# A feed-forward's bias product in four row groups, gelus in pairs, and a new order of its pipelined step

## The chip, the core and the metric

The kernel runs on one NeuronCore of a Trainium2 chip. The metric is the device time of one execution in microseconds (us), the median of several runs. The core has five engines that matter here, each with its own instruction stream: TensorE (PE in the profile; its weight loads are PEld), VectorE (DVE), ScalarE (ACT), GpSimd (POOL) and SyncE (SP, which issues DMAs). [...]

## The reference

Two blocks are applied to x of 8 x 256 x 512. The first adds a convolution-like mixing and then a quantised feed-forward; the second adds a cross attention and a mixture of experts. The change is in the feed-forward of the first block:

```python
def _activation_quant(x):
    scale = 127.0 / jnp.clip(jnp.max(jnp.abs(x), axis=-1, keepdims=True), EPS_ACT)
    return jnp.clip(jnp.round(x * scale), -128, 127) / scale
def _bitlinear(x, w, b):
    xn = _layer_norm(x)
    xq = _activation_quant(xn)
    wq = _weight_quant(w)          # round(w / scale) in {-1, 0, 1}, times scale
    return jnp.einsum('bsd,fd->bsf', xq, wq) + b
h = _bitlinear(x, w1, b1)          # 512 -> 2048
h = jax.nn.gelu(h, approximate=False)
return _bitlinear(h, w2, b2)       # 2048 -> 512
```

So each row is normalised, rounded to integers with a scale of its own, multiplied by a ternary matrix, given a bias, put through a gelu, and then the same again with the second matrix.

## The kernel before

The 2048 rows stay in SBUF as 16 tiles of 128 rows (xs). The kernel has stages: the mixing (to about 193 us of the profiled span), the feed-forward (to about 337 us), the attention, and the experts.

**The feed-forward** works on pairs of tiles, `Pair` (L286), pairs 0 to 7. A pair goes through these methods, each of which issues instructions on one or two engines:

- `moments` (L296, VectorE; the root on GpSimd, `root` L274), `rounded` (L305, VectorE): centres the rows, finds the largest, scales and rounds into xc. L315 is its last instruction.
- `split` (L360, GpSimd): the bias has to be added ahead of a multiplication by the row's scale s1, so it is divided by it: u = 1/s1 is split into three bf16 parts, the bias b1 also (`bias_parts` L240), and the nine products of parts are a matmul of nine rows. The parts of u go to u9 (L366), those of b1 to b1k.
- `turn_x` (L373): eight transposes on TensorE (L171, written as f_xT), moved to xq by ScalarE (L376). `turn_u` (L378): u9 transposed (L382), moved to ub by ScalarE (L384).
- `product(i, half)` (L397): for tile i of the pair and one half (1024 columns) of the hidden layer, eight matmuls (L404) and then two of the bias (L411), into hp, a PSUM tile of two banks. Its tag "conv" has two buffers.
- `gelu(i, half)` (L416, ScalarE): hp to hs in SBUF, with the row sums as a by-product in hsum (L417; it shows as two rows, the second an ACTIVATION_READ_ACCUMULATOR). `hidden` is product and gelu.
- `mean` (L422): from the sums the mean of the gelu's rows, two small VectorE instructions (hm, L425 and L115); then ScalarE centres hs[1] (L427). `centre` (L429): VectorE centres hs[0] (L431).
- `squares` (L435, ScalarE, L439) and `largest` (L443, VectorE, L444) for each tile; `scales` (L448; VectorE, root on GpSimd); `scales_back` (L454, VectorE); `rounded_back` (L460, VectorE, two instructions L462).
- `turn_back(i, half)` (L467): eight transposes (L171, f_hT) and their eviction by ScalarE (L479).
- `back(i)` (L484): sixteen matmuls of the second product (L488). `update(i)` (L493, VectorE, L496) adds it to xs; `add_bias` (L498, two GpSimd adds of the second bias, L500).

**What sets the order.** Everything from L752 to L1211 lies in `in_order(tc)` (L58): on TensorE, VectorE, ScalarE and GpSimd each, instructions run in the order in which the program issues them. So the order is written by hand. Pairs are pipelined: in step g of the loop at L1079 the pair `p` = g has its hidden layer computed, `mid` = g - 1 has its hidden layer's scale computed, `last` = g - 2 goes through the second product, `left` = g - 3 has its last tile finished, and `coming` = g + 1 is normalised and rounded. Pairs 0 and 1 have a run-in ahead of the loop (L1014 to L1078). Step 8 has an order of its own (L1111 to L1146), in which the attention begins; step 9 is the last.

In step g (2 < g < 8) the order ends with these calls, and then comes `left.back(1)` of the next step:

```python
        if p:
            p.hidden(1, 1)
        if mid:
            mid.scales_back()
        prepare(3)
        if coming:
            coming.turn_x()
        if p:
            p.mean()
        if mid:
            mid.rounded_back()
```

PSUM holds, beside "conv", two buffers of "tr" (all transposes) and two of "mm" (second product).

The parts of b1 are brought to b1k by DMAs that ScalarE's queue issues (L248, L251), in the mixing stage: its loop over 16 groups of heads (L779) calls `next(bias_rows)` in groups 9, 10 and 12 (L813).

## Time and profile before

| | |
|---|---|
| runs (3) | median 1145.42 us, 1143.35 to 1147.33 |
| the profiled execution's own time | 1143.72 us |
| its span, first to last instruction | 1141.9 us |
| mean granted clock of TensorE | 0.995 |
| busy, share of the span: PE, PEld, DVE, ACT, POOL | 96%, 58%, 60%, 46%, 39% |
| 0 to 190 us: PE, DVE, ACT, POOL busy | 170.63, 168.71, 100.00, 144.96 |
| 190 to 345 us: PE, DVE, ACT, POOL busy | 147.21, 130.07, 127.39, 62.13 |
| L404: matmuls, busy, mean | 256, 61.8 us, 386 ns |
| L411: matmuls, busy, mean | 64, 19.5 us, 387 ns |
| L417: gelus, busy, mean | 32, 38.5 us, 1204 ns |
| L251: DMAs issued, median time to issue | 3, 282 ns |

The span is counted from the first to the last instruction; times inside it are from its start. Matmuls are pipelined, so one that lasts 386 ns starts 216 ns after the one before it; a sum is made from start to start. "Idle before" is what an engine waited ahead of an instruction, with the instruction that ended the wait.

### The profile page before, as it was taken

To read this page: it belongs to the slowest core of one execution; us is meant where nothing else is said; L and a number is where in the kernel's file an instruction comes from. 1 tells how busy PE (TensorE), PEld (TensorE's weight loads), DVE (VectorE), ACT (ScalarE), POOL (GpSimd) and SP (SyncE) were. 2 spreads that over 40 slices of the span, in tenths; PEclk is the share of its full clock that TensorE was granted. 3 is DMA by queue.
4 is the path that set the end of the run, shared out by engine and by line. 5 is a ranking of instruction groups with operands and counts; after the bars stand their busy time and mean duration, and the time that the engine had idled before them with its cause. 6 is when DMAs were issued, how large, how long until landed. Compare 5 with 4: busy or idle time off the path is not lost.

```text
span 1141.9 us, 16502 instructions
## 1 busy us (share of the span) xinstructions
PE 1099.7 (96%) x5885; PEld 662.1 (58%) x5885; DVE 686.2 (60%) x1507; ACT 519.6 (46%) x1173; POOL 443.0 (39%) x501
## 2 busy tenths in 40 slices
PE   4999998899999999999999998999999999999997
PEld 3777776445545555555555555654466676675443
DVE  5998999898866565765757657637612222212452
ACT  4437645788984555656556566621011121111000
POOL 5787887225531243433434334412770000000650
PEclk9999999999999999999999999999999999999999
DMA  8424520799500100000000010052669999997571
GB/s 272 156 75 143 162 75 20 239 307 290 145 1 19 38 1 1 20 20 1 20 7 13 2 37 1 1 195 93 239 217 297 303 329 338 299 315 231 157 248 40
DMA packets 122780, 153.26 MB, mean 134 GB/s; under 512 B 7481, under 2 KB 81273, under 8 KB 122178
## 3 DMA queue, kind: packets, MB, share of 16 engines
q1 hardware_dynamic: 108608, 116.49, 32.2%
q10 hardware_dynamic: 8962, 18.85, 4.6%
q0 software_dynamic: 5120, 16.78, 4.4%
q8 instruction: 49, 0.80, 0.3%
q14 instruction: 41, 0.34, 0.1%
HBM read 107.66 MB, written 44.43 MB: 133 GB/s over the span
## 4 chain that ended last, share of the span: by engine, by line
PE 75%; DVE 18%; ACT 2%; POOL 2%; issue 2%; DMA 0%; ACTq 0%; POOLq 0%; DVEq 0%
PE r_h L1726 10%; PE gu L1541 10%; PE y L708 5%; PE v_mm L880 5%; PE r_po L1742 5%; PE q_mm L880 5%; PE po L1563 5%; PE f_op L488 4%; PE pt L1281 4%; PE k_mm L880 3%; PE f_hp L404 3%; PE fo L1312 3%; DVE mx L1253 2%; PE sc L1245 2%; PE o L1300 2%
## 5 line engine op out<-in xcount | busy, mean ns | idle before, releaser
L1270 POOL TENSOR_TENSOR pr<-pr,rden 128x1024 f32<-128x1024 f32 x64 | 121.1, 1893 | 218.9 <-DVE rden L1268 212.4
L708 PE MATMUL y<-kv,tp 128*128 128x288 f32 x640 | 161.7, 409 | 5.2 <-DVE wl L731 5.1
L708 PEld LDWEIGHTS y<-kv,tp 128*128 128x128 f32 x640 | 119.3, 190 | 42.3 <-PE y L708 10.1
L1261 ACT ACTIVATE pr<-sc,mx 128x256 f32<-128x256 f32 x256 | 118.3, 483 | 8.2 <-DVE mx L1253 7.2
L1884 POOL DMA_INDIRECT yg<-yd,slot x32 | 33.4, 1043 | 222.2 <-PE gu L1541 204.4
L1726 PE MATMUL r_h<-r_xT,r_gu 128*128 128x256 f32 x512 | 113.5, 380 | 0.0
L1726 PEld LDWEIGHTS r_h<-r_xT,r_gu 128*128 128x128 f32 x512 | 97.1, 190 | 20.4 <-issue 8.0
L1253 DVE TENSOR_REDUCE mx<-sc 128x4 f32<-128x1024 f32 x64 | 77.5, 1213 | 4.8 <-PE sc L1245 4.8
L1733 DVE SCALAR_TENSOR_TENSOR r_y<-r_h,eb,r_ge 128x256 f32<-128x256 f32 x32 | 15.5, 484 | 95.5 <-PE r_h L1726 95.5
L1281 PE MATMUL pt<-ident,pr 128*128 128x128 f32 x512 | 70.5, 281 | 2.3 <-POOL pr L1270 1.4
L1286 ACT COPY pts<-pt 128x512 f32<-128x512 f32 x64 | 37.8, 590 | 68.2 <-PE pt L1281 68.1
L1281 PEld LDWEIGHTS pt<-ident,pr 128*128 128x128 f32 x512 | 55.8, 142 | 20.1 <-issue 15.1
L404 PE MATMUL f_hp<-w1q,f_xq 128*128 128x512 bf16 x256 | 61.8, 386 | 5.5 <-ACT f_h L417 2.9
L1732 ACT ACTIVATE r_ge<-r_h,gb 128x256 f32<-128x256 f32 x32 | 15.1, 473 | 108.9 <-PE r_h L1726 108.9
L646 POOL TENSOR_TENSOR kv<-kx 128x2048 f32<-128x2048 f32 x16 | 57.6, 3600 | 12.8 <-ACT kx L632 12.8
L1312 PE MATMUL fo<-Wo_sb,oT 128*128 128x512 f32 x128 | 58.0, 596 | 1.2 <-ACT oT L1304 1.1
L880 PE MATMUL k_mm<-Wk_sb,cx 128*128 128x512 f32 x128 | 58.1, 598 | 0.6
L488 PE MATMUL f_op<-w2q,f_hq 128*128 128x512 bf16 x256 | 57.9, 379 | 0.0
L880 PE MATMUL v_mm<-Wv_sb,cx 128*128 128x512 f32 x128 | 57.7, 594 | 0.0
L1742 PE MATMUL r_po<-r_w,r_y 128*128 128x512 f32 x128 | 57.7, 594 | 0.0
L880 PE MATMUL q_mm<-Wq_sb,xT 128*128 128x512 f32 x128 | 57.6, 593 | 0.0
L1553 ACT ACTIVATE ge<-gu,gb 128x512 f32<-128x512 f32 x16 | 11.0, 687 | 100.6 <-PE gu L1541 98.0
(486 smaller groups left out, 2114.4 us busy)
## 6 DMA issues: line engine op xcount, KB each, us to landing
xd<-blank SPq DMA_DIRECT2D x1, 15360.0 KB, 59.5
tp<-kpd SPq DMA_DIRECT2D x32, 256.0 KB, 3.3
r_gu<-in_rg SPq DMA_DIRECT2D x16, 512.0 KB, 6.4
r_gu<-in_rw SPq DMA_DIRECT2D x16, 512.0 KB, 6.6
r_w<-in_rw SPq DMA_DIRECT2D x16, 512.0 KB, 6.7
r_xr<-xd SPq DMA_DIRECT2D x16, 512.0 KB, 6.7
yd<-r_yo ACTq DMA_DIRECT2D x32, 256.0 KB, 5.7
yd<-blank SPq DMA_DIRECT2D x1, 6144.0 KB, 78.3
```

The costliest lines, as they stand in the source:

```text
L404: nc.tensor.matmul(dst, lhsT=self.xq[:, i, c, :], rhs=w1q[:, c, cols], start=(c == 0), stop=False)
L488: nc.tensor.matmul(op, lhsT=self.hq[i][:, c, :], rhs=w2q[:, c, :], start=(c == 0), stop=(c == FC - 1))
L708: nc.tensor.matmul(y[:, ll, :, 0:PAIRS], lhsT=tp[:, dl : dl + P], rhs=view(kv, (m0 * G + hh) * PAIRS, [[G * PAIRS, B], [1, PAIRS]]), start ...
L880: nc.tensor.matmul(t, lhsT=lT[:, c, i * P : (i + 1) * P], rhs=w[:, c, :], start=(c == 0), stop=(c == DC - 1),)
L1253: nc.vector.tensor_reduce(self.mx, self.sc.rearrange("p r c k -> p (r c) k"), AX.X, ALU.max, negate=True)
L1261: nc.scalar.activation(self.pr[:, h // 2, h % 2, :], self.sc[:, h // 2, h % 2, :], AF.Exp, bias=self.mx[:, h : h + 1], accum_out=self.den[ ...
L1270: nc.gpsimd.tensor_tensor(flat, flat, rden.unsqueeze(2).to_broadcast([P, 4, S]), ALU.mult)
L1281: nc.tensor.transpose(pt[:, cc, k, :], self.pr[:, rr, cc, k * P : (k + 1) * P], ident)
L1312: nc.tensor.matmul(fo, lhsT=oT[:, c, :], rhs=wsb["Wo"][:, c, :], start=(c == 0), stop=(c == DC - 1))
L1541: nc.tensor.matmul(ps, lhsT=w[0][:, c, k, f * P : (f + 1) * P], rhs=xTs[tb][:, c, :], start=(c == 0), stop=(c == DC - 1),)
L1726: nc.tensor.matmul(ps, lhsT=self.w[0][:, c, k, f * P : (f + 1) * P], rhs=self.xT[:, c, 0:n], start=(c == 0), stop=(c == DC - 1),)
L1742: nc.tensor.matmul(po, lhsT=self.y[:, f, i * P : (i + 1) * P], rhs=self.w[1][:, f, :], start=(f == 0), stop=(f == EC - 1),)
```

## The change

- **Bias parts.** Before, the nine rows of parts lie in partitions 0 to 8 and the bias product of each 512 columns is a matmul over all 128 partitions. After, the nine rows of b1k for columns 512 r to 512 r + 511 lie in partitions 32 r to 32 r + 8 (r = 0 to 3), u9 holds its nine rows four times, 32 apart, and `parts(i)` issues four matmuls of 32 rows each, one per group of 32 rows of the array, each into a PSUM bank of its own. All four of a tile come together, after both halves of the tile. GpSimd writes u9 with two small copies per part, where it was one; the DMAs to b1k are twelve smaller ones where there were three, in groups 11, 12 and 13 of the mixing.
- **A tile's halves.** `product(i, 0)` and `product(i, 1)` both precede `parts(i)`, so both buffers of "conv" belong to one tile. `gelu(i)` issues the tile's two gelus one after the other.
- **The step.** `turns` and the interleaving inside a product are gone. `parts(0)` and `gelu(0)` follow `last.turn_back(0, 1)`; `mid.squares(1)` follows them; `product(1, 0)` follows `last.back(0)`, then `last.turn_back(1, 1)`; `product(1, 1)` and `parts(1)` come where `hidden(1, 1)` was; `gelu(1)` comes after `coming.turn_x()`. Pairs 0 and 1 are rewritten in the same way.

```diff
         for i in range(3):
-            nc.scalar.dma_start(b1k[3 * i : 3 * i + 3, :], b1d)
+            for r in range(4):
+                row = 32 * r + 3 * i
+                nc.scalar.dma_start(b1k[row : row + 3, bass.ts(r, D)], b1d[:, bass.ts(r, D)])
+            yield
...
-                nc.gpsimd.tensor_copy(
-                    u9[:, :, 3 * j : 3 * j + 3],
-                    up[:, j, :].unsqueeze(2).to_broadcast([P, 2, 3]),
-                )
+                for i in range(2):
+                    nc.gpsimd.tensor_copy(
+                        u9[:, i, :].rearrange("p (r k) -> p r k", r=4)[:, :, 3 * j : 3 * j + 3],
+                        up[:, j, i : i + 1].unsqueeze(2).to_broadcast([P, 4, 3]),
+                    )
...
+        def product(self, i, half):
+
+            if half == 0:
+                self.hp = []
             hp = pp.tile([P, FF // 2], F32, tag="conv", name=f"{self.nm}_hp{i}{half}")
-            self.hp = hp
+            self.hp.append(hp)
...
+        def parts(self, i):
+
+            for r in range(4):
+                rows = slice(32 * r, 32 * r + 32)
                 nc.tensor.matmul(
-                    hp[:, q * D : (q + 1) * D], lhsT=self.ub[:, i, :], rhs=b1k[:, cols],
-                    start=False, stop=True,
+                    self.hp[r // 2][:, bass.ts(r % 2, D)], lhsT=self.ub[rows, i, :],
+                    rhs=b1k[rows, bass.ts(r, D)], start=False, stop=True,
                 )
...
+        def gelu(self, i):
+            for half in range(2):
+                nc.scalar.activation(
+                    self.hs[i][:, bass.ts(half, FF // 2)], self.hp[half], AF.Gelu, bias=zero,
+                    scale=self.s1[:, i : i + 1], accum_out=self.hsum[:, i, half : half + 1],
+                )
+
+        def hidden(self, i):
+
+            for half in range(2):
+                self.product(i, half)
+            self.parts(i)
+            self.gelu(i)
...
-        if g in (9, 10, 12):
+        if g in (9, 10, 11, 12, 13):
             next(bias_rows, None)
...
-    one.hidden(0, 0)
-    one.hidden(0, 1)
+    one.hidden(0)
...
-    one.hidden(1, 0)
+    one.product(1, 0)
     more_mixed()
-    one.hidden(1, 1)
+    one.product(1, 1)
+    one.parts(1)
+    one.gelu(1)
...
-    two.hidden(0, 0)
+    two.hidden(0)
     three.moments()
     one.largest(0)
     one.squares(0)
-    two.hidden(0, 1)
     three.rounded()
     three.split()
-    two.hidden(1, 0)
+    two.product(1, 0)
...
     two.product(1, 1)
+    two.parts(1)
     one.scales_back()
     three.turn_x()
     three.turn_u()
-    two.gelu(1, 1)
+    two.gelu(1)
...
-        def turns():
-
+        if p:
+            p.product(0, 0)
             if g > 2:
                 p.turn_u()
-            mid.squares(1)
-            if g > 2:
-                last.turn(0, 0)
-
-        if p:
-            p.hidden(0, 0, turns)
-        if g == 2:
-            p.hidden(0, 1)
-        if g == 2 or not p:
-            last.turn(0, 0)
-        last.turned(0, 0)
+            else:
+                p.product(0, 1)
+                p.parts(0)
+                p.gelu(0)
+        last.turn_back(0, 0)
...
         if p and g > 2:
-            p.hidden(0, 1)
+            p.product(0, 1)
         last.turn_back(0, 1)
...
-        if p:
-            p.hidden(1, 0)
+        if p and g > 2:
+            p.parts(0)
+            p.gelu(0)
+        if mid:
+            mid.squares(1)
         last.turn_back(1, 0)
         last.back(0)
+        if p:
+            p.product(1, 0)
+        last.turn_back(1, 1)
...
-        last.turn_back(1, 1)
         if p:
-            p.hidden(1, 1)
+            p.product(1, 1)
+            p.parts(1)
         if mid:
             mid.scales_back()
         prepare(3)
         if coming:
             coming.turn_x()
         if p:
+            p.gelu(1)
             p.mean()
```

More of the change, by code (lines that the diff above doesn't have):

```diff
@@ L390, in turn_u @@
             self.hsum = stat.tile([P, 2, 2], F32, tag="hsum", name=nm + "_hsum")
-        def hidden(self, i, half, between=None):
-            self.product(i, half, between)
-            self.gelu(i, half)
-        def product(self, i, half, between=None):
+        def product(self, i, half):
+            if half == 0:
+                self.hp = []
             hp = pp.tile([P, FF // 2], F32, tag="conv", name=f"{self.nm}_hp{i}{half}")
-            self.hp = hp
+            self.hp.append(hp)
             for q in range(2):
                 cols = bass.ts(2 * half + q, D)
-                dst = hp[:, q * D : (q + 1) * D]
                 for c in range(DC):
                     nc.tensor.matmul(
-                        dst, lhsT=self.xq[:, i, c, :], rhs=w1q[:, c, cols], start=(c == 0), stop=False
-                    )
-            if between:
-                between()
-            for q in range(2):
-                cols = bass.ts(2 * half + q, D)
+                        hp[:, bass.ts(q, D)], lhsT=self.xq[:, i, c, :], rhs=w1q[:, c, cols],
+                        start=(c == 0), stop=False,
+                    )
+        def parts(self, i):
+            for r in range(4):
+                rows = slice(32 * r, 32 * r + 32)
                 nc.tensor.matmul(
-                    hp[:, q * D : (q + 1) * D], lhsT=self.ub[:, i, :], rhs=b1k[:, cols],
-                    start=False, stop=True,
-                )
-        def gelu(self, i, half):
-            nc.scalar.activation(
-                self.hs[i][:, bass.ts(half, FF // 2)], self.hp, AF.Gelu, bias=zero,
-                scale=self.s1[:, i : i + 1], accum_out=self.hsum[:, i, half : half + 1],
-            )
+                    self.hp[r // 2][:, bass.ts(r % 2, D)], lhsT=self.ub[rows, i, :],
+                    rhs=b1k[rows, bass.ts(r, D)], start=False, stop=True,
+                )
+        def gelu(self, i):
[9 more added lines that the diff above has]
+            self.gelu(i)
         def mean(self):
```

## The prediction, made before the change was run

> **What bounds the kernel now.** I read the busy shares first (TensorE 96%), then the table of busy times by stretch for the feed-forward steps, and then the timelines of the engines inside one step. The table (us; then busy us and instruction counts of TensorE, its weight loads, VectorE, ScalarE, GpSimd; then granted clock, DMA share, GB/s) has for one step of the loop:

> ```profile
> 263.80:282.10 18.30, 18.28 (x116) 9.54 (x115) 16.54 (x32) 16.22 (x19) 8.23 (x21) 1.00 1.05 289
> ```

> TensorE is full: a step lasts 18.30 us because its matmuls do. But VectorE has 16.5 and ScalarE 16.2 of the same 18.30, so a saving on TensorE is worth little before another engine is late. What that engine is, the timelines of VectorE and ScalarE say (start, us, instruction, idle before it):

> ```profile
> 275.15 0.87 DVE L315 TENSOR_SCALAR f_xc<-f_xc,f5q_qs 128x512 f32<-128x512 f32 x2
> 278.00 0.16 DVE L266 TENSOR_TENSOR f3hq_a<-f_hmax,f3h_r 128x2 f32<-128x2 f32 x1 [1.24 <-POOL f3h_r L283]
> 278.81 0.15 DVE L425 TENSOR_TENSOR f_hm<-f_hsum 128x2 f32<-128x2 f32 x1
> 279.10 2.47 DVE L462 TENSOR_SCALAR f_h<-f_h,f3hq_qs 128x2048 f32<-128x2048 f32 x2
> 292.82 0.88 DVE L315 TENSOR_SCALAR f_xc<-f_xc,f6q_qs 128x512 f32<-128x512 f32 x2
> ```
> ```profile
> 276.48 1.20 ACT L417 ACTIVATE f_h<-f_hp,zero,f_s 128x1024 f32<-128x1024 f32 x1 [0.54 <-PE f_hp L411]
> 277.58 0.19 ACT L417 ACTIVATION_READ_ACCUMULATOR f_h<-f_hp,zero,f_s 128x1 f32 x1
> 277.67 1.10 ACT L376 ACTIVATE f_xq<-f_xT,nhalf 128x1024 bf16<-128x1024 f16 x1
> 279.27 2.00 ACT L427 ACTIVATE f_h<-f_h,f_hm 128x2048 f32<-128x2048 f32 x1 [0.49 <-DVE f_hm L115]
> ```

> VectorE's own round: rounding of the coming pair (L315, ends 276.02), L425 (hm, which needs the gelu's sums) 2.8 later, and 14.9 from hm to the end of the next rounding (278.81 to 293.70). Together 17.7, under 18.3, and hm does not wait: the last gelu's sum is there at 277.77, a microsecond early, because that gelu runs **ahead** of xq (L376).

> **The change, part by part.**

> *Bias parts in row groups.* Before, a tile's four bias matmuls cost 4 x 0.216 = 0.86 (L411: two in 0.43, start to start). The scores of the later attention are four 32-row matmuls side by side:

> ```profile
> 414.25 3.60 PE L1312 MATMUL fo<-Wo_sb,oT 128*128 128x512 f32 x8
> 417.78 1.15 PE L1245 MATMUL sc<-kT_T,qT_T 32*128 32x256 f32 x16
> 418.85 1.09 PE L1281 MATMUL pt<-ident,pr 128*128 128x128 f32 x8
> ```

> The sixteen take 1.07 to the next start; sixteen at full height and this width would take 3.49 (eight of twice the width, L880, take 3.49). So four cost about 1.23 of one, and four bias matmuls about 0.27; the ends are 0.22 and 0.86. TensorE is spared 0.59 a tile, 9.5 us over 16 tiles; a step of two tiles then needs 17.1.

> The scores begin 0.04 after the last full-height matmul should end (414.25 + 3.49). [...] At 0.04 a switch, 32 switches would cost 1.3 of the 9.5; no more than that can be read off this trace.

> *Nine more small DMAs (L251)* on ScalarE's queue, 0.28 each: 1.1 us more in each of two groups of the mixing stage, 0.3 in a third. ScalarE idles there 1.8 to 6.6 us a group before the next kx copy (waiting for its DMA), which hides them; without that cover it is 2.5 at most. Nothing is gained. I take 0. They land long before 196 us, the first use.

> *GpSimd's split:* 11 instructions instead of 8. At its measured starts (L365 to L371, 0.15 to 0.26 apart) it lasts 2.1 instead of 1.7, and starts 1.9 after the rounding's end (295.58 against 293.70), so it ends at 4.1. Behind it stands the bias add L500.

> *The new order of the step: the part that decides.* L417's last two gelus are now issued **after** the coming pair's turn_x. ScalarE runs in program order, so they queue behind xq, xq behind the eight transposes, and these behind the rounding. hm waits for both gelus, and VectorE's 14.9 us of work stand behind hm. So a new ring closes. From the rounding's end R:

> - to the transposes' start 0.1; from there to xq 0.65 (208.42 to 209.07);
> - xq to gelu 0.99 (220.14 to the next start, 221.13);
> - two gelus with the second's sum 2.45 (below: 227.99 to 230.44), to hm 0.03: hm at R + 4.2, where it was R + 2.8;
> - hm to the next rounding's end 14.9.

> ```profile
> 227.99 1.18 ACT L417 ACTIVATE f_h<-f_hp,zero,f_s 128x1024 f32<-128x1024 f32 x1
> 229.17 1.19 ACT L417 ACTIVATE f_h<-f_hp,zero,f_s 128x1024 f32<-128x1024 f32 x1
> 230.25 0.19 ACT L417 ACTIVATION_READ_ACCUMULATOR f_h<-f_hp,zero,f_s 128x1 f32 x1
> ```

> **19.1 us a round.** TensorE, at 17.1, now stands 2 us in each step in front of the transposes L171. ScalarE keeps up: its last square ends 0.1 to 1.5 us before xq can start.

> *A collision.* The add L500 follows the split, at R + 4.1; hm comes at R + 4.2. What the two do to each other is in this pair of rows, GpSimd's and VectorE's:

> ```profile
> 241.37 1.26 POOL L500 TENSOR_TENSOR xs<-xs,b2b 128x512 f32<-128x512 f32 x1
> ```
> ```profile
> 241.39 1.27 DVE L115 SCALAR_TENSOR_TENSOR f_hm<-f_hm,ones 128x2 f32<-128x2 f32 x1
> ```

> A 0.16 us instruction took 1.27, until the add ended. If this happens in each round, it is 20.2 (add's end 5.35, second hm 0.2, then 14.6 from L462 on). If the split ends later than the ring assumes (ScalarE's square late by 0.5), its last small casts are pushed between the two L462 and the add behind the next L431, as at 281.58, at no cost. I take two rounds of each; the ends are four of 19.1 and four of 20.2. [...]

> *Four rounds* (hm of pair 3 to hm of pair 6 count from that of pair 2, g = 3 to 6; after that no pair is coming). Before: L425 at 241.19 and 314.45, 73.3. After: 2 x 19.1 + 2 x 20.2 = 78.6. **+5.3** (+3.1 to +7.5).

> *Run-in.* Pairs 0 and 1 gain about 0.4 at the start, where VectorE's adds L624 set the pace. Then both gelus of a tile run together, so the next tile's first half finds its PSUM buffer taken (TensorE waits 1.4 at 213.8), pair 0's two squares end at 220.3 (were at 220.2), and xq, ub, two gelus follow: hm of pair 1 at 224.0 (was 223.5). In g = 2 the gelus and two evictions (2.36 + 2.0) now stand ahead of the square of hs[1], and the square of hs[0] behind the eviction of the last transposes: it ends 239.4, then xq 1.0 and gelus 2.45, hm at 242.8. This is at full clock. Before, a pause of 2.63 halved the clock for what followed:

> ```profile
> 229.31 3.23 PE L404 MATMUL f_hp<-w1q,f_xq 128*128 128x512 bf16 x8 [2.63 <-ACT f_h L417]
> ```

> and 1.7 us went. After, the pause is 2.2; the price is 0 to 1.7, I take half. hm of pair 2 at 243.6: **+2.4** (+1.6 to +3.3).

> *Run-out.* In g = 7 nothing is coming, the gelus wait for the square alone, and hm of pair 7 comes 17.5 to 18.0 after that of pair 6 (was 333.81 - 314.45 = 19.4): **-1.4** (to -1.9). From there, g = 8 and all later stages are the same code and move as a block.

> **Sum.** 2.4 + 5.3 - 1.4 = +6.3. The profiled execution took 1143.72 (span 1141.9, 1.8 around it), so it would take 1150.0; the median of the runs is 1145.42, 1.7 above it, and with the same shift I forecast **1151.7**. Its ends are +2.8 and +9.7.

> **Rivals.**

> - *Faster.* TensorE's spared time is collected: VectorE runs its own round of 17.7, TensorE needs 17.1, and each of four steps falls from 18.3 to 17.7, with 1.2 more in g = 7: -3.6, 1141.8. For it: no idle of TensorE in five steps, and every step it gives back is on the chain of waits. It decides if hm comes within 3.1 us of the rounding's end; the rows make it 4.2, since xq and the two gelus alone are 3.4. Chance 0.12.
> - *No change (within 0.3%, 3.4 us, about what a measurement of this kernel can tell).* The ring holds at 19.1 with no collision, and the run-in is hidden, for VectorE has waits of 1.9 (L266 at 222.70) to spare: 0 to 0.5 + 3.1 - 1.9, about +1.5, 1146.9. Chance 0.16.
> - *Worse.* The collision in each round, and the clock halved after each pause: transposes 0.45 later in four rounds, 9.7 + 1.8 = +11.5, 1156.9. For it: the pause is 2 to 3 us, at the 2.63 that halved it once. Chance 0.12.
> - *The row groups do not run side by side.* TensorE then needs 18.3 a step, still under 19.1, and the time is the forecast's; it is no separate case.

> The forecast itself has 0.60. Slower by over 0.3%: 0.60 + 0.12 = 0.72; same 0.16; faster 0.12. The range from 1146.0 to 1157.0 leaves out the faster case and little else.

> **What would show it.** Right: L376 ahead of two L417 in ScalarE's row, L425 idle 1.4 us or longer with ACT f_h L417 as its releaser (before: 0.57, once), transposes L171 of f_xT preceded by 2 us of idle TensorE released by DVE f_xc L315, steps of 19 to 20.3, L411 four at a time in about 0.3. Wrong: TensorE without gaps from 245 on, or steps under 18.3; or hm early, which would mean that ScalarE's order is not what I read from the code. The collision shows as an L425 or L115 of 1.2 us beside L500; the clock as a granted clock under 0.9 in the steps.

## The result, and the profile after

After the change the kernel takes **1159.9 us** (median of 4 runs, 1157.89 to 1162.25); the kernel before, beside it, 1144.49. The ratio is 1.0128, with a 95% interval of 1.0110 to 1.0146: slower, as forecast, but by 15.4 us where 6.3 were forecast, and outside the range that was given. The profiled execution took 1162.25, the longest of the four; its span is 1160.5, TensorE's mean granted clock 0.992.

Landmarks of the two profiled executions (start, us from the span's start; hm is L425 before and L437 after) say where the time comes from. A pair's hm marks the middle of its step, so hm to hm is one round of the loop; the run-in is what lies ahead of hm of pair 2, the run-out is from hm of pair 6 to hm of pair 7:

| | before | after | moved by | the prediction |
|---|---|---|---|---|
| hm of pair 2 | 241.19 | 246.78 | +5.6 | +2.4 |
| hm of pair 6 (four rounds) | 314.45 | 325.73 | +11.3 | +7.7 |
| hm of pair 7 | 333.81 | 344.81 | +11.0 | +6.3 |
| first xTp of the attention | 343.3 | 355.8 | +12.5 | +6.3 |
| rank, start of the routing | 781.2 | 792.1 | +10.9 | +6.3 |
| first r_h, end of the routing | 842.3 | 860.9 | +18.6 | +6.3 |

**The rounds.** One round of the loop, hm to hm, in the table of busy times by stretch (columns as before):

```profile
265.69:285.76 20.07, 17.81 (x116) 8.82 (x115) 17.16 (x33) 16.54 (x19) 9.88 (x28) 1.00 1.05 289
```

TensorE is no longer full: 17.81 of 20.07. The timelines of VectorE, ScalarE, GpSimd and TensorE around that hm, in this order (start, us, instruction, idle before it and what ended it):

```profile
280.87 0.88 DVE L319 TENSOR_SCALAR f_xc<-f_xc,f5q_qs 128x512 f32<-128x512 f32 x2
...
285.76 1.25 DVE L437 TENSOR_TENSOR f_hm<-f_hsum 128x2 f32<-128x2 f32 x1 [1.15 <-ACT f_h L422]
```
```profile
282.24 1.11 ACT L381 ACTIVATE f_xq<-f_xT,nhalf 128x1024 bf16<-128x1024 f16 x1 [1.10 <-PE f_xT L171]
283.25 1.20 ACT L422 ACTIVATE f_h<-f_hp,zero,f_s 128x1024 f32<-128x1024 f32 x1
...
284.43 1.20 ACT L422 ACTIVATE f_h<-f_hp,zero,f_s 128x1024 f32<-128x1024 f32 x1
```
```profile
285.72 1.27 POOL L512 TENSOR_TENSOR xs<-xs,b2b 128x512 f32<-128x512 f32 x1
```
```profile
279.67 0.39 PE L415 MATMUL f_hp<-b1k,f_ub 32*128 32x512 bf16 x4
281.41 0.79 PE L171 MATMUL f_xT<-ident,f_xc 128*128 128x128 f16 x8 [1.35 <-DVE f_xc L319]
```

This is the ring as forecast: rounding (ends 281.7), transposes, xq, two gelus, hm, which waits 1.15 for the second gelu. Then the collision: GpSimd's add has started 0.04 before hm, and hm takes 1.25 in place of 0.15. This is not a wait ahead of an instruction, as the 1.15 is, but an instruction that lasts 1.1 longer: GpSimd's add held VectorE up without a wait.

The rounds are 18.9, 20.1, 20.0 and 20.0, 79.0 in all (forecast 78.6; before 73.3). The hm of 1.25 above lengthens the round that starts with it, and so does the next one; these are the third and the fourth. The round shown, the second, is long for another reason, near its start (VectorE, then GpSimd):

```profile
268.43 2.37 DVE L443 TENSOR_SCALAR f_h<-f_h,f_hm 128x2048 f32<-128x2048 f32 x1
```
```profile
268.45 1.27 POOL L512 TENSOR_TENSOR xs<-xs,b2b 128x512 f32<-128x512 f32 x1
```

Here the split was late, and the add came behind it, the outcome that the prediction put at no cost. But the centring L443 took 2.37 in place of 1.28 beside the add. In the first round the split was late too, and there the add took 2.31 and L443 its usual 1.27. The rows of the two rounds differ by one more VectorE instruction ahead of L443 in the second (L1100, 0.15, which only g = 4 has); that it decides who is held up is not shown. The kernel before has the same 2.37 in that step (L431 at 262.72).

**The clock.** TensorE in g = 2, then in g = 8:

```profile
223.12 5.30 PE L406 MATMUL f_hp<-w1q,f_xq 128*128 128x512 bf16 x16 [2.66 <-ACT f_h L422]
...
232.32 0.61 PE L171 MATMUL f_hT<-ident,f_h 128*128 128x128 f16 x8 [2.57 <-ACT f_hq L491]
232.77 5.30 PE L500 MATMUL f_op<-w2q,f_hq 128*128 128x512 bf16 x16
```
```profile
346.42 1.03 PE L171 MATMUL f_hT<-ident,f_h 128*128 128x128 f16 x8 [3.08 <-DVE f_h L474]
347.25 4.77 PE L892 MATMUL k_mm<-Wk_sb,cx 128*128 128x512 f32 x8
```

Sixteen such matmuls take 3.62 at full clock and these eight take 3.65 (both are shown below, in the changed kernel's second execution). The granted clock is 0.50 from 224.5 to 226.5, from 234 to 236 and from 347.3 to 349, and 1.00 in all four rounds. So three pauses, of 2.66, 2.57 and 3.08, are each followed by 1.5 to 1.7 us of lost time on TensorE.

**The run-out.** Nothing is coming in this step, and still two of VectorE's small instructions stand beside an add (GpSimd's adds start at 325.69 and 342.90):

```profile
325.73 1.24 DVE L437 TENSOR_TENSOR f_hm<-f_hsum 128x2 f32<-128x2 f32 x1 [1.15 <-ACT f_h L422]
...
342.98 1.20 DVE L270 TENSOR_TENSOR f6hq_a<-f_hmax,f6h_r 128x2 f32<-128x2 f32 x1 [1.26 <-POOL f6h_r L287]
```

**The end.** In the routing VectorE has two long waits (7.44 ahead of L1581 at 835.81, which the profile puts down to TensorE, and 6.96 at 845.61, put down to something outside the core) that it does not have in the profile before. That code is the same in both kernels; whether the wait belongs to the change was a question for the runs.

### The profile page after: what moved, and what is told of

It reads as the page before. It is cut to its first block, busy times and chain, and to the rows that moved or that the text cites. A ratio compares the mean times of both kernels' runs of the same rounds, so it can differ in the third digit from the quotient of the medians.

```text
span 1160.5 us, 16538 instructions
## 1 busy us (share of the span) xinstructions
PE 1097.9 (95%) x5885; PEld 656.7 (57%) x5885; DVE 688.9 (59%) x1507; ACT 520.7 (45%) x1173; POOL 440.7 (38%) x525
## 4 chain that ended last, share of the span: by engine, by line
PE 69%; DVE 21%; ACT 4%; POOL 2%; issue 2%; another core or an unknown queue 1%; DMA 0%; ACTq 0%; POOLq 0%; DVEq 0%
PE r_h L1740 10%; PE gu L1555 10%; PE y L720 5%; PE v_mm L892 5%; PE r_po L1756 5%; PE q_mm L892 5%; PE po L1577 4%; PE k_mm L892 3%; PE pt L1295 3%; PE fo L1326 3%; PE f_op L500 2%; DVE mx L1267 2%; PE sc L1259 2%; PE f_hp L406 2%; PE o L1314 2%
## 5 line engine op out<-in xcount | busy, mean ns | idle before, releaser
L500 PE MATMUL f_op<-w2q,f_hq 128*128 128x512 bf16 x256 | 59.6, 387 | 0.0
L1555 PE MATMUL gu<-xT,s_gu 128*128 128x512 f32 x128 | 56.2, 594 | 0.0
```

What stands on the lines that cost most here:

```text
L500: nc.tensor.matmul(op, lhsT=self.hq[i][:, c, :], rhs=w2q[:, c, :], start=(c == 0), stop=(c == FC - 1))
L1555: nc.tensor.matmul(ps, lhsT=w[0][:, c, k, f * P : (f + 1) * P], rhs=xTs[tb][:, c, :], start=(c == 0), stop=(c == DC - 1),)
```

## The experiments

In all, 15 kernels ran, in four groups on four chips, each beside the kernel before (1141.88, 1145.22, 1142.07 and 1145.22 us). "Rounds" is hm of pair 2 to hm of pair 6.

**The changed kernel again.** No edit.

> The changed kernel itself once more, beside the other experiments. After the feed-forward its product of rank came 10.9 us later than in the kernel before, but the whole execution took 18.5 us more, because the routing stage waited 7.4 and 7.0 us on VectorE for transfers of rows (dxs), which four other executions with the same stage did not do. If that wait belongs to one run and not to the change: 1152 to 1155, rank to first r_h 61 us, ratio about 1.010. If it belongs to the changed kernel: 1158 to 1162 again, and rank to r_h 68 to 69.

1158.4 (1155.36 to 1158.63), ratio 1.0106 (1.0086 to 1.0127): the loss is there again. From rank to r_h 64.5: neither 61 nor 68. All four kernels of that chip had 64.5 to 66.7, the one with the order of before too (h, below, 65.0); all eight on two other chips had 61.1 or 61.2, whatever their order. And the kernel before without its bias adds (o, below), on a fourth chip, shows the same wait (VectorE):

```profile
814.21 0.75 DVE L1553 SCALAR_TENSOR_TENSOR yT<-gu,eb,ge 128x512 f32<-128x512 f32 x1 [6.23 <-remote]
826.74 0.69 DVE L1566 TENSOR_TENSOR xs<-xs,po 128x512 f32<-128x512 f32 x1 [9.67 <-remote]
```

The medians of the kernel before agree: 1141.88 and 1142.07 on the two chips with 61.1 or 61.2, 1145.22 on both of the others. So these waits vary between chips and executions, and are not the change's. The clock varies too: the same pauses as above, in this execution of the same kernel, cost nothing in two cases of three (the first was followed by 5.30 again):

```profile
232.88 0.61 PE L171 MATMUL f_hT<-ident,f_h 128*128 128x128 f16 x8 [2.58 <-ACT f_hq L491]
233.32 3.62 PE L500 MATMUL f_op<-w2q,f_hq 128*128 128x512 bf16 x16
...
345.37 0.62 PE L171 MATMUL f_hT<-ident,f_h 128*128 128x128 f16 x8 [3.09 <-DVE f_h L474]
345.83 3.65 PE L892 MATMUL k_mm<-Wk_sb,cx 128*128 128x512 f32 x8
```

**c: dummy matmuls in the three pauses.**

```diff
+    def warm(n, name):
+        ps = pp.tile([P, D], F32, tag="mm", bufs=2, name=name)
+        for _ in range(n):
+            nc.tensor.matmul(ps, lhsT=w1q[:, 0, 0:P], rhs=w1q[:, 0, 0:D], start=True, stop=True)
...
+        if g == 2:
+            warm(11, "warm0")
         if p:
             p.product(0, 0)
...
+        if g == 2:
+            warm(10, "warm1")
         last.turn_back(1, 0)
...
             left.back(1)
+            warm(12, "warm2")
             mid.centre()
```

> The changed kernel with matmuls that nobody reads put into three pauses of TensorE: eleven ahead of the first product of g = 2, ten ahead of the third group of transposes of g = 2, twelve ahead of the first transposes of g = 8 (0.22 us each). Theory: these pauses of 2.6, 2.6 and 3.1 us halve TensorE's clock, which costs 1.8, 1.7 and 1.5 us after them; kept busy, the clock stays full and the time falls by 4 to 5 us, to 1155 to 1156; the first product of g = 2 lasts 3.5 for sixteen instead of 5.3, hm of pair 2 comes 3.4 earlier than 246.8. Rival (the run-in is late because of its order alone, the clock is covered by waits): within 1 us of 1159.9.

1149.9, ratio 1.0073 (1.0056 to 1.0091); hm of pair 2 comes 3.5 earlier than in the first profile after, first xTp at 350.8, 5.0 earlier than in the first and 2.5 earlier than in the second. The product behind the dummies is at full speed:

```profile
220.18 2.54 PE L1025 MATMUL warm<-w1q 128*128 128x512 bf16 x11
223.01 3.62 PE L406 MATMUL f_hp<-w1q,f_xq 128*128 128x512 bf16 x16 [0.29 <-ACT f_h L422]
```

So the clock costs the changed kernel up to 5 us in an execution. With it gone hm of pair 2 is at 243.30, 2.1 later than before, where the prediction's terms without the clock make +1.6; 1.4 of the 2.1 lies between hm of pair 1 and that of pair 2 (19.1 against 17.7).

**d: the kernel before, with nothing but both gelus of tile 1 behind turn_x.**

```diff
         if p:
-            p.hidden(1, 0)
+            p.product(1, 0)
+            hp0 = p.hp
...
-            p.hidden(1, 1)
+            p.product(1, 1)
+            hp1 = p.hp
...
             coming.turn_x()
         if p:
+            p.hp = hp0
+            p.gelu(1, 0)
+            p.hp = hp1
+            p.gelu(1, 1)
             p.mean()
```

> The kernel before (bias at full height, old order), with one part of the change alone: the two gelus of a pair's second tile are issued after the coming pair's turn_x. Theory of the ring: hm at 4.2 us after the rounding's end instead of 2.8; the four rounds grow from 73.3 to between 76.4 and 81, and the time from 1144.5 by 2 to 8 us, to 1146.5 to 1152.5, with hm waiting for the gelu in each of steps 3 to 6. Rival (the order of these gelus is harmless, the loss comes from the rest of the new order): within 1.5 us of 1144.5.

1147.01, ratio 1.0039 (1.0025 to 1.0053). Rounds 77.7 in place of 73.3, and hm waits for the gelu and for an add:

```profile
283.42 0.85 DVE L425 TENSOR_TENSOR f_hm<-f_hsum 128x2 f32<-128x2 f32 x1 [1.16 <-ACT f_h L417]
```

The late gelus alone, in the old order and at full-height bias parts, and the collision that they bring (0.7 in three of the rounds), make most of the loss in the rounds (4.4 of 5.7).

**a: the changed kernel with tile 1's gelus ahead of turn_x.**

```diff
             p.parts(1)
+            p.gelu(1)
...
             coming.turn_x()
         if p:
-            p.gelu(1)
             p.mean()
```

> The changed kernel, but in the loop the gelus of a pair's second tile are issued right after their bias parts, ahead of the coming pair's turn_x (the old place); all else as changed. Theory (ring: rounding, transposes, xq, two gelus, hm, VectorE's 14.9 us): the ring opens, VectorE's own round of 17.7 or TensorE's 17.1 bounds, so the four rounds from hm of pair 2 to hm of pair 6 fall from 79.0 to 71 to 73.5, hm no longer waits for a gelu, and the time falls by 6 to 9 us from the changed kernel's 1159.9, to 1151 to 1154. Rival (the halved TensorE clock in g = 2 and g = 8 and the small GpSimd copies made the loss, not the order): rounds stay at 19 to 20 and the time within 2 us of 1159.9.

1154.06, ratio 1.0106 (1.0089 to 1.0123): almost nothing is won. hm no longer waits, but the rounds are 19.7, where the rival had them. TensorE, then VectorE, show a second ring, which my theory lacked:

```profile
288.22 0.46 PE L387 MATMUL f_uT<-ident,u 128*128 128x128 f32 x2 [1.62 <-POOL u L371]
```
```profile
300.98 0.16 DVE L119 SCALAR_TENSOR_TENSOR f4h_ve<-f_hss,ln_eps 128x2 f32<-128x2 f32 x1 [1.93 <-ACT f_junk L451]
```

ScalarE's square of hs[0] now ends last; behind it come GpSimd's root, and behind that the split, whose last small operations each take 1.1 to 1.3 beside VectorE's roundings in place of 0.2 to 0.3. So turn_u is late, and with it ub, both evictions, parts(0), the gelus and again the square.

**b: four bias matmuls at full height, in the changed order.**

```diff
-                    self.hp[r // 2][:, bass.ts(r % 2, D)], lhsT=self.ub[rows, i, :],
-                    rhs=b1k[rows, bass.ts(r, D)], start=False, stop=True,
+                    self.hp[r // 2][:, bass.ts(r % 2, D)], lhsT=self.ub[:, i, :],
+                    rhs=b1k[:, bass.ts(r, D)], start=False, stop=True,
```

> The changed kernel, but the four bias matmuls of a tile run at full height, all 128 rows, one after the other (the other rows of b1k are zero, so the sum is the same). Theory of the ring: TensorE stands 1.3 to 2 us in each late round in front of the transposes, so 0.55 us more per tile is hidden in the loop; rounds of 18.9 to 20.1 as before, time within 3 us of 1159.9 (the run-in and the run-out may pay for some tiles). Rival (the row groups are worth what they spare on TensorE): 16 x 0.55 = 9 us slower, 1169.

1153.73, ratio 1.0100 (1.0080 to 1.0120), rounds 79.4, against 79.0 in both executions of the changed kernel: while the rings set the pace, the row groups are worth 0.1 a round.

**h: the row groups in the order of before,** two at a time.

```diff
-                    hp[:, q * D : (q + 1) * D], lhsT=self.ub[:, i, :], rhs=b1k[:, cols],
+                    hp[:, q * D : (q + 1) * D], lhsT=self.ub[32 * r : 32 * r + 32, i, :],
+                    rhs=b1k[32 * r : 32 * r + 32, bass.ts(r, D)],
```

> The kernel before, its order kept, with nothing of the change but the bias parts in row groups: two at a time, beside each other, behind each half's product. Two side by side take 0.24 to 0.28 where two at full height took 0.43: 0.3 to 0.4 us a step and half of it a tile, so 0.6 to 0.7 a step of TensorE's 18.3. Theory: the steps are bound by TensorE, so that rounds 3 to 6 fall from 18.3 to 17.7 (VectorE's own round of 17.7 is next), and the time falls by 2 to 3.5 us, ratio 0.997 to 0.998. Rival: VectorE or the split (11 casts instead of 8, which push the add) is late instead, and nothing is gained or 1 to 2 us lost.

1146.23, ratio 1.0010 (0.9992 to 1.0028), rounds 73.7 (18.4 each). Nothing is gained, as the rival had it, but not for the rival's reason: TensorE is still full (18.3 of 18.4 us of a round). Its rows show why:

```profile
286.15 1.89 PE L408 MATMUL f_hp<-w1q,f_xq 128*128 128x512 bf16 x8
287.97 0.39 PE L416 MATMUL f_hp<-b1k,f_ub 32*128 32x512 bf16 x2
288.29 0.62 PE L171 MATMUL f_hT<-ident,f_h 128*128 128x128 f16 x8
```

The product takes 1.82 to the start of the parts (1.73 before, when full-height matmuls followed), and two parts 0.32, where the two of before took 0.43: 2.14 against 2.16. Four together, in the changed kernel, take the same 0.32 to 0.33 (291.19 to 291.51). So two at a time save nothing, and four at a time 4.32 less 3.88 (1.73 + 1.82 + 0.33), 0.44 a tile.

**e and l: the adds moved in the changed kernel.** In e `left.add_bias()` comes after `coming.moments()`; l only turns the two adds round:

```diff
-            for T in self.T:
+            for T in self.T[::-1]:
                 nc.gpsimd.tensor_tensor(T, T, b2b, ALU.add)
```

> The changed kernel with GpSimd's two bias adds issued after the coming pair's moments, so that no add stands behind the split when hm comes. Theory of the collision (in three of four rounds an add holds VectorE's 0.16 us instruction for 1.25): these three rounds fall from 20.0 to 18.9, hm of pair 6 and all later landmarks come 3 us earlier, and hm lasts 0.15. Rival, found in the kernel with the gelu first: a second ring through the square of hs[0], its root on GpSimd and the split holds the rounds near 19.7 whatever the add does: then at most 1 us is won.

> The changed kernel with nothing but the order of GpSimd's two adds turned round: tile 1's first. It must wait for the update of tile 1, so both run some 6 us after hm, beside VectorE's statistics, which the trace shows at their usual 0.68 beside such an add, and not beside the 2x tensor_scalars. Theory of the collision: three rounds of 20.0 become 18.9, hm lasts 0.15, hm of pair 6 and rank come 3.3 us earlier than in the same kernel with the old order. Rival: the second ring (square of hs[0], root, split, turn_u) is as long as the first: 1 us or less.

e: 1161.72, ratio 1.0136 (1.0105 to 1.0168), rounds 83.2 (20.8 each): slower, which neither side expected. l, against its theory too, gains almost nothing in the rounds: 1150.66, ratio 1.0077 (1.0060 to 1.0094), rounds 78.8 (19.7 each), and the round after them 17.0 where it was 19.1. VectorE, in e and in l:

```profile
299.23 2.69 DVE L313 TENSOR_SCALAR f_xc<-xs,f_mv 128x512 f32<-128x512 f32 x2
```
```profile
292.89 0.94 DVE L119 SCALAR_TENSOR_TENSOR f6a_ve<-f_mv,ln_eps 128x2 f32<-128x2 f32 x1
```

The collision moved: from hm and L443 (1.1 longer) to the centring L313 (1.8) and to L119 (0.8). Each time the round is 18.9 plus that price: 20.0, 20.8, 19.7; and in d, with 0.7 on hm, 19.6.

**m and o: no adds at all,** in the changed kernel and in that before (`add_bias` issues nothing).

> The changed kernel without the two bias adds on GpSimd (the second bias of the feed-forward is left out). Theory: a round is the ring of 18.9 through ScalarE's late gelus and hm, plus what an add costs VectorE where it stands (beside hm 1.1: 20.0; beside the coming pair's L119 0.8: 19.7; beside the centring L313 1.8: 20.8). Without any add all four rounds are 18.8 to 19.0, hm of pair 6 is 75.2 to 76.0 after that of pair 2 (79.0 with the adds), and the time is 3 to 5 us under that of the changed kernel on the same chip. Rival: the second ring, through the split and turn_u, takes over: rounds of 19.5 or more.

> The kernel before without the bias adds. Its adds cost VectorE nothing that its rounds of 18.3 show (hm took 0.15 in all of them, and TensorE stood full): rounds 18.2 to 18.3 as before and the same time within 1 us. If its time falls by 3 us as well, the adds are a price of both kernels and explain nothing of the change.

Both leave the second bias out of the result. m: 1151.6, ratio 1.0040 (1.0024 to 1.0056), rounds 18.9, 19.0, 18.9, 18.9, in all 75.7: the ring without the collision. (ScalarE's square of hs[0] ends there only as xq starts, 299.17 and 299.10, so the second ring is about as long, and 18.9 does not tell the two apart.) o: ratio 0.9996 (0.9978 to 1.0013), rounds 73.3: before, the adds cost nothing. So of the 5.7 us lost in four rounds 3.3 (79.0 less 75.7) are the collision and 2.4 the ring.

**f, i, j, n: both rings opened.** f is a, with the split ahead of the root and the adds placed as in e. i is a, with the square of hs[0] ahead of the eviction hq10 and the adds as in l:

```diff
+        if mid and p:
+            mid.squares(0)
         last.turn_back(1, 0)
...
         last.turn_back(1, 1)
-        if mid and p:
-            mid.squares(0)
```

> The changed kernel with three moves: tile 1's gelus ahead of turn_x, the split ahead of the root of the square sums on GpSimd, the bias adds after the coming moments. Theory of two rings: with the gelu first alone, the rounds stayed at 19.7, since the split was late (stuck between VectorE's roundings), turn_u 1.6 and ScalarE 2.1 us late with it. With the split ahead of the root, ub is ready when product(0, 0) is, and the second ring falls by 1.5: rounds of 18.0 to 18.5, near the 17.7 of VectorE's own round, and a time 5 to 6 us under that of the gelu-first kernel: 1147.5 to 1149.5. Rival: the second ring is set by the two gelus and evictions ahead of the square of hs[0] on ScalarE and not by the split: rounds stay at 19.5 or more, time 1153.

> The changed kernel with three moves that leave GpSimd's order alone: tile 1's gelus ahead of turn_x, the square of hs[0] ahead of the third eviction hq10 (so the root and the split behind it on GpSimd start 2 us earlier and end before VectorE's roundings), and the bias add of tile 1 ahead of that of tile 0 (so both adds run after the update beside the statistics, and none beside hm or the roundings). Theory of two rings and a collision: rounds 18.2 to 18.7 in place of 20.0, hm of pair 6 near 319, that of pair 7 near 338, rank at 785 to 787 where the changed kernel had 789.6 and 792.1. Rival: with the packed parts TensorE and ScalarE have a ring of their own of 19 or more, since both halves of a tile must be ready before either gelu: rounds stay at 19.2 or more and rank at 789 or later. The time: ratio 1.003 to 1.006, if the theory holds.

> The kernel above with dummy matmuls in the pauses of g = 2 and g = 8, so that the clock is not halved there (it was worth 5 us in the changed kernel). If the loss consists of the two rings, the collision and the clock, nearly all of it is gone: rank at 780 to 783 (before: 781.2), ratio 0.998 to 1.002. If something else of the change costs time, the ratio stays above 1.003.

> Tile 1's gelus ahead of turn_x, the square of hs[0] ahead of hq10, and no bias adds (left out as above). With the adds this order gave rounds of 18.5 and 19.2 in turn. Theory: the 0.7 to 0.8 between them is the add beside L119; without it the rounds are 18.0 to 18.5, bound by ScalarE's chain from hm by the rounding and both evictions to the two gelus (6.8 + 11.4 = 18.2), and not by TensorE, whose work is 17.6 a step. Rival: TensorE's spared time comes through, rounds of 17.6 to 17.9, which would say that the new order can be faster than the old one of 18.3.

f: 1163.87, ratio 1.0151 (1.0118 to 1.0184), rounds of 21.1, the last of 22.1: my plan failed in a way that neither side expected. The adds cost L313 its 1.8 as in e, and the root now waits behind the split, so that VectorE idles longer than in a:

```profile
264.74 0.16 DVE L270 TENSOR_TENSOR f2hq_a<-f_hmax,f2h_r 128x2 f32<-128x2 f32 x1 [2.83 <-POOL f2h_r L287]
```

i: 1144.86, ratio 1.0027 (1.0017 to 1.0036), rounds 18.5, 19.2, 18.5, 19.2. This takes back most of the loss with three moves. j, the dummies added: ratio 1.0031 (1.0019 to 1.0042), against the expected 0.998 to 1.002. Its run-in is 3.4 shorter, but 1.4 is lost in the round of pair 7 (19.2 where i had 17.8), and the dummies of g = 8 take longer than the pause they fill, so that hT starts 2.7 after hm where in i it was 1.6. n, without adds: ratio 1.0013 (0.9996 to 1.0029), rounds 18.1, 17.9, 19.1, 17.8, in all 72.8. The rounds of 17.8 and 17.9 are the rival's: TensorE is busy for 17.3 of them, so its spared time does come through, until in one round the split's last copies meet the rounding (GpSimd's copies L371 at 281.88 take 2.34 for two, and turn_u waits 0.87).

**k: the kernel before with eleven dummies ahead of product(1, 0) of g = 2.**

> The kernel before with eleven dummy matmuls ahead of product(1, 0) of g = 2, in its one pause of 2.63 us, behind which eight matmuls took 3.23 and two bias matmuls 0.98. If the pause halves the clock: these take 1.89 and 0.60, and hm of pair 2 and all later landmarks come 1.7 us earlier (239.5 and 779.5), ratio 0.997 to 1.000. If the pause is not what slows them, nothing changes.

1140.63, ratio 0.9991 (0.9982 to 1.0001). The eight matmuls take 1.89 in place of 3.23, as expected, but hm moves by 0.7 only (17.0 after that of pair 1, before 17.7): with the gelu early it no longer waits, and VectorE's own chain sets it. No version was shown to beat the kernel before.

## Why the prediction was right and where it was wrong

The ring inside the rounds held, and the collision with hm. What failed is the clock term of the run-in, with the step that everything after pair 7 moves as a block: one pause was priced, at half of 1.7, where TensorE had three, and lost 1.7, 1.7 and 1.5 behind them. The run-out failed by 1.1 besides, because two adds were left out of it.

- *Four rounds, +5.3: right,* +5.7. The ring of 19.1 is 18.9, taken without the collision in m. "Two rounds of each" was so for hm, which met an add in two of the four. But the other outcome, "at no cost", cost 1.1 in one of its two rounds, where the add stood beside L443. That the sum still came within 0.4 is in part luck, since both kinds of round were put 0.2 too long.
- *Run-in, +2.4: its clock term failed.* "The price is 0 to 1.7, I take half" counted one pause. There are two, of 2.66 and 2.57, and in this execution both cost 1.7 on TensorE. VectorE's wait for the square of hs[0] grew to 4.89 at 243.41 (1.51 in c, where the pauses are filled), and hm of pair 2 came 5.6 late. From hm of pair 1 to pair 2 the clock cost 3.4 in this execution and 1.7 in the second, where 0.85 was taken. Without the clock the step was about right (c: +2.1, the terms +1.6).
- *Run-out, -1.4: wrong,* -0.3. "The gelus wait for the square alone" was so, but two adds were left out: hm of pair 6 meets one (1.24), and L270 at 342.98 meets one (1.20 for 0.16). That is 2.1 of the 19.1; in l, where neither meets one, the round is 17.0. Taking the adds away is not enough, though: in m the round is 18.4, for hm comes before the split is done, whose last two copies (L371 at 321.91) then take 2.41 beside VectorE's rounding and make turn_u late.
- *"From there, g = 8 and all later stages are the same code and move as a block": wrong twice.* The pause ahead of hT in g = 8 is 3.08 now, and the clock was halved there too: +1.5. And the same code does not take the same time in each execution: from xTp to rank the profiled execution before took 437.9, with a granted clock of 0.91 from 700 to 720 us, and all others 436.3; and the routing took 7.7 longer after. With these (12.5 less 1.6, and 7.7) the two profiles' difference of 18.6 at r_h is made up.
- *Rivals.* "The row groups do not run side by side" was no case; they do, four in 0.33 rather than 0.27. "Faster" needed hm within 3.1 us of the rounding; n shows that some of it can be collected, if both rings are opened and the adds are out of the way: 72.8 over four rounds against 73.3. "Worse", with its clock halved after a pause, was nearest, though the pauses that counted lie outside the rounds: those within are 1.35 to 1.6, and after them the second product L500 kept its 3.62.
- *The sum.* Of 6.2 us missing in the feed-forward (12.5 less 6.3), 3.2 are the run-in, 0.4 the rounds, 1.1 the run-out, 1.5 step 8. The medians differ by 15.4; what they show beyond 12.5 is of the size of the waits in the routing, but only one of these executions has a profile, so that is not shown. Up to the first xTp the change costs 10.0 and 12.5 in its two profiles, by how often the clock is halved. The forecast's upper end, +9.7, is 0.3 more than its own terms make (3.3 + 7.5 - 1.4).

The prediction's row for the adds showed what one does to a small instruction; what was missing was to look for every other instruction that an add of 1.27 would meet in its new place.

Open: what decides whether the clock is halved after a pause of 2 to 3 us; and why the routing waits longer on some chips.

## What to carry to other kernels

Where the chains of several engines are nearly as long as the work of the full one (here 17.7 of VectorE beside 18.3 of TensorE), an order has several rings of nearly one length; take one off, and the next one holds, so list for each engine what it waits for last, and what that waits for. A small instruction on VectorE is not small beside a GpSimd pass (hm took 1.25 for 0.15 beside an add of 1.27): place such passes by what runs beside them, and price the place they are moved to as well. Each new pause of TensorE, in a single step too, has to be priced with a clock that may be halved behind it: here pauses of 2.04 to 3.08 were followed by 1.4 to 2.9 us of lost time, though not in every execution, and those of 1.35 to 1.69 in the rounds by none.
